# Rotary step of a second attention: the half exchange moved into the product, one addition for two, and new scheduling orders

## Chip, cores and metric

The kernel runs on one core of one Trainium2 chip. The metric is the device time of one execution in microseconds (us), the median of three runs. The profile is one further execution taken by the hardware profiler.

## What is computed

The reference handles 16 sequences of 256 tokens and 256 channels, all in float32. It adds four blocks to the input `x` in turn:

```
x = x + attention0(cross_attention(x, fside))         # 16 heads of 16, rotary, causal
x = x + feed_forward0(selected_linear(x))             # FP4-like quantisation by blocks of 16
x = x + attention1(diffusion(x))                      # 16 heads of 64, rotary, segments of 128
x = x + mixture_of_experts(conditioned(x))            # 8 experts, top 2, and a shared one
```

The change concerns the rotary step of `attention1`:

```
q = q * cos + rotate_half(q) * sin      # rotate_half: (t0, t1) -> (-t1, t0), pair by pair
k = k * cos + rotate_half(k) * sin
```

The weights are laid out so that the first elements of all pairs stand in one half (`r = 0`) and the second elements in the other (`r = 1`). With the halves a and b the result is `a*cos - b*sin` and `b*cos + a*sin`.

## The kernel before

The first three blocks are written as generators, one for each stage and engine-independent: `stage_h`, `stage_i` (cross attention), `stage_a`, `stage_m`, `stage_x`, `stage_e` (first attention), `stage_y`, `stage_f` (feed forward; `stage_gate`, `stage_up`, `stage_down` quantise its weights at the start), `stage_d` (diffusion), `stage_p`, `stage_k`, `stage_u` (queries, keys, values of the second attention), `stage_s`, `stage_g`, `stage_v` (its scores, exponentials and values). Each stage loops over the 16 sequences, and the second attention over four groups of four heads within each. The fourth block (`mixture`) is ordinary code that follows.

A planner, `weave`, interleaves the stages while the program is built. It keeps a modelled clock for each engine, asks every stage for its next operation, and issues the one that can start first. Between operations that can start equally early on the same engine, the table `ORDER` decides: it ranks the stages for each engine (PE, DVE, ACT, POOL, and SP, which issues the DMAs). So a changed cost or rank moves instructions on every engine, while their number and sizes stay the same, with two exceptions. An operation that may run on ACT or DVE (`copy_`) can change its engine. And where the modelled PE would stand idle by more than `GAP`, and a multiplication of the identity by itself into a free PSUM bank fits ahead of the next real one with a `MARGIN` of 0.2 us, the planner puts that in (`kept_warm`); its result is not used. In this text these are the fillers; in the profile they are `single<-ident` with no second operand, two matrix instructions each.

The second product and the two additions stand in `turned4`, which `stage_p` and `stage_k` call 64 times each. PE writes both halves of a projection into one bank `pq`, DVE makes `t1 = pq * cos` and `t2 = pq * sin`, both 128x512, POOL combines them in two instructions of 128x256, and SP issues four DMAs of 64 KB which bring the halves into the interleaved places of `f_q` or `keys`. `stage_s` then multiplies `f_q` and `keys` on PE. All of the woven operations carry the line L186 in the profile, that of the helper that records them; in it `single` and `pair` are PSUM tiles, `f_t1q`, `f_t2q`, `f_t1k` and `f_t2k` the products, `b_e` and `f_prob` the probabilities of the two attentions, `c_y` and `d_h` the rows that are quantised in the feed forward.

Of the kernel before, what the change touches and what calls it, by code (L numbers as in the profile page):

```python
# [13 lines left out]
F32 = mybir.dt.float32  # L14
# [3 lines left out]
ALU = mybir.AluOpType  # L18
AX = mybir.AxisListType

P = 128
S = 256
# [89 lines left out]
class Op:  # L112
# [14 lines left out]
SIDE = {32: 0.125, 64: 0.2}  # L127
TURN = 0.01
XBUFS = 7
GAP = 0.6  # L130
MARGIN = 0.2
SLACK = {"PE": 0.0, "DVE": 0.05, "ACT": 0.1, "POOL": 0.02, "SP": 0.0}
EARLY = 200.0, 0.2
EASE = 1.5
ORDER = {
    "PE": "h y down a i m f s e g v d p gate c k x u up",
    "DVE": "d v f c h i x e a g k up gate p down u s m y",
    "ACT": "f p up h i k y gate m e a v d u g x c s down",
    "POOL": "m f h i e a y v down x g s d u up gate k p c",
    "SP": "v x a h i f p g s m d gate y u up k e c down",  # L140
}
BANK_LATER = {"PE": None, "DVE": True, "ACT": True, "POOL": None, "SP": None}

# [71 lines left out]
def weave(streams, spare):  # L215
# [64 lines left out]
    while waiting:  # L280
# [36 lines left out]
        waiting = [w for w in waiting if w[0] is not None]  # L317
        if best is not None and best[2][0] == "PE" and best[2][2] and best[3] > free.get("PE", 0.0) + GAP:
            op = spare()
# [29 lines left out]
def mm_(g, out, pairs, start=True, stop=True):  # L349

    last = len(pairs) - 1
    for i, (lhsT, rhs) in enumerate(pairs):
        yield g.pe.matmul(out, lhsT, rhs, start=start and i == 0, stop=stop and i == last)


def copy_(g, dst, src):

    a, v = g.act.copy(dst, src), g.dve.tensor_copy(dst, src)
    return Op(a.choices + v.choices, a.outs, a.ins)
# [42 lines left out]
def load(g, pool, name, shape, src):  # L402

    t = pool.tile(shape, F32, name=name)
    return t, g.sp.dma_start(out=t, in_=src)
# [12 lines left out]
def single(g, *ins):  # L418

    return (yield Want(g.singles, ins))  # L420
# [269 lines left out]
def row32(j, n):  # L690
    return slice(32 * j, 32 * j + n)
# [328 lines left out]
def tile_l(g, shape, name, bufs=1, tag=None):  # L1020
    return g.l_.tile(shape, F32, name=name, tag=tag or name, bufs=bufs)


def stage_p(g):
    k, a = g.k, g.a
    yield lambda: g.done["A"] > 0 and g.done["W"] == 3 and g.done["T"] > 2 * max(OTHER) + 1


    g.z = []
    for n in ("condB_zX", "condB_zY", "condB_zR"):  # L1030
        t, op = load(g, g.w, n, [P, g.B], a[n].unsqueeze(0).to_broadcast([P, g.B]))
        g.z.append(t)
        yield op

    g.iota, op = load(g, g.w, "iota", [16, 1], a["iota"][0:16])
    yield op
    idxf = g.w.tile([16, g.B], F32, name="idxf")
    yield g.dve.tensor_copy(idxf, k.idx[0:16, 2, :])
    yield g.dve.tensor_scalar(k.onehot, idxf, g.iota, None, ALU.is_equal)

    zc = g.w.tile([P, g.B], F32, name="zc")
    yield g.dve.tensor_tensor(zc, g.z[0], g.z[1], ALU.add)
    yield g.dve.scalar_tensor_tensor(zc, zc, -2.0, g.z[2], ALU.mult, ALU.add)
    yield g.dve.tensor_scalar(g.z[2], g.z[2], -1.0, None, ALU.mult)
    g.z.append(zc)
    g.gn, op = load(g, g.w, "g", [P, 2], a["g"])
    yield op
    g.cos1, op = load(g, g.w, "cos1", [P, S], a["cos1"])
    yield op
    g.sin1, op = load(g, g.w, "sin1", [P, S], a["sin1"])  # L1050
    yield op

    g.pmo = g.w.tile([P, 2, D], F32, name="pmo")
    pmv = tile_l(g, [P, 2, 2, 2 * P], "wq", 2)
    yield g.sp.dma_start(out=pmv, in_=a["pmv"].rearrange("p c (r w) -> p c r w", r=2))
    for c in range(2):
        wo = tile_l(g, [P, 4, D], "wq", 2)
        yield g.sp.dma_start(out=wo, in_=a["w_out1"][:, 4 * c : 4 * c + 4, :])
        pmvT = tile_l(g, [P, 4, P], "f_pT", 3)
        one = yield from single(g, pmv)  # L1060
        pt = one.rearrange("p (i t) -> p i t", i=4)
        for i in range(4):
            yield g.pe.transpose(pt[:, i, :], pmv[:, c, i // 2, (i % 2) * P : (i % 2 + 1) * P], g.ident)
        yield copy_(g, pmvT, pt)
        g.singles.append(one)
        one = yield from single(g, pmvT, wo)
        pm = one[:, :D]
        yield from mm_(g, pm, [(pmvT[:, i, :], wo[:, i, :]) for i in range(4)])
        yield copy_(g, g.pmo[:, c, :], pm)
        g.singles.append(one)  # L1070

    g.keys = [g.w.tile([P, 2, 2, PM + P], F32, name=f"keys{n}") for n in range(4)]
    part = tile_l(g, [P, 2, S], "f_t1q").rearrange("p r s -> p (r s)")[:, : 8 * PM]
    part = part.rearrange("p (n a m) -> p n a m", n=4, a=2)
    for h in range(4):
        for r in range(2):
            src = a["pmk"][row32(h, 32), :, r, h * PM : (h + 1) * PM]
            dst = part[64 * (h % 2) + r : 64 * (h % 2) + 64 : 2, :, h // 2, :]
            yield g.sp.dma_start(out=dst, in_=src)
    for n in range(4):  # L1080
        yield g.pool.tensor_copy(g.keys[n][:, :, :, 0:PM], part[:, n].unsqueeze(2).to_broadcast([P, 2, 2, PM]))
    g.mhalf = g.w.tile([P, 2], F32, name="mhalf")
    yield g.pool.memset(g.mhalf, -0.5)
    g.done["Z"] = 1
    g.wq, g.queries = {0: (yield from fetch_p(g, 0))}, {}
    for i in range(4 * g.B):
        yield lambda: g.done["D"] > i // 4 and i < g.done["S"] + 2 and g.done["K"] >= i
        if i + 1 < 4 * g.B:
            g.wq[i + 1] = yield from fetch_p(g, (i + 1) % 4)
        q = g.queries[i] = tile_l(g, [P, 2, S], "f_q", 2)  # L1090
        move = lambda half, a, src: g.sp.dma_start(out=q[half, a, :], in_=src)
        yield from turned4(g, g.zT[i // 4], g.wq[i][:, 0], "q", DH1**-0.5, move)
        g.done["P"] = i + 1


def stage_k(g):

    yield lambda: g.done["Z"]
    by_seg = lambda t: t.rearrange("p (s t) -> p s t", s=2)
    for i in range(4 * g.B):  # L1100
        yield lambda: g.done["D"] > i // 4 and i < g.done["S"] + 4 and i in g.wq
        keys = g.keys[i % 4]
        move = lambda half, a, src: g.sp.dma_start(out=keys[half, a, :, PM:], in_=by_seg(src))
        yield from turned4(g, g.zT[i // 4], g.wq[i][:, 1], "k", None, move)
        g.done["K"] = i + 1
# [49 lines left out]
def fetch_p(g, n):  # L1155

    wq = tile_l(g, [P, 2, 2, 2 * P], "wq", 2)
    for which in range(2):
        cols = slice((8 * which + 2 * n) * P, (8 * which + 2 * n + 2) * P)
        yield g.sp.dma_start(out=wq[:, which], in_=g.a["w_qk1"][:, :, cols])  # L1160
    return wq
# [31 lines left out]
def turned4(g, zT, w, name, scale, move):  # L1193

    one = yield from single(g, w, zT)
    pq = one.rearrange("p (r t) -> p r t", r=2)
    for r in range(2):
        yield from mm_(g, pq[:, r, :], [(w[:, c, r * P : (r + 1) * P], zT[:, c, :]) for c in range(2)])
    t1, t2 = tile_l(g, [P, 2, S], f"f_t1{name}"), tile_l(g, [P, 2, S], f"f_t2{name}")
    for t, by in ((t1, g.cos1), (t2, g.sin1)):  # L1200
        table = by.unsqueeze(1).to_broadcast([P, 2, S])
        if scale is None:
            yield g.dve.tensor_tensor(t, pq, table, ALU.mult)
        else:
            yield g.dve.scalar_tensor_tensor(t, pq, scale, table, ALU.mult, ALU.mult)
    g.singles.append(one)
    yield g.pool.tensor_tensor(t1[:, 0, :], t1[:, 0, :], t2[:, 1, :], ALU.subtract)
    yield g.pool.tensor_tensor(t1[:, 1, :], t1[:, 1, :], t2[:, 0, :], ALU.add)
    for a in range(2):
        for r in range(2):  # L1210
            yield move(slice(r, P, 2), a, t1[64 * a : 64 * a + 64, r, :])
# [632 lines left out]
```

## Time and profile before

| | us |
|---|---|
| median of three runs (2489.93 to 2493.80) | 2491.32 |
| the profiled execution | 2491.22 |
| its span, from first to last instruction | 2489.5 |
| PE busy, share of the span | 2447.2, 98% |
| DVE, ACT, POOL busy | 1345.4, 1205.1, 1061.1 |
| end of the woven part, by its last PE instruction | 1523.6 |

The page gives busy time by engine and in 40 slices of the span. Matrix instructions overlap, and their ends are modelled; where the space from one start to the next matters, it is taken from the trace's starts. A group's line gives out<-in, shapes, count, the busy time of the group, the mean ns of one, and then the idle time of the engine ahead of them with what ended most of it.

### The profile page before, as it was taken

What the parts mean: (1) busy time and instruction counts of PE and PEld (TensorE: products, weight loads), DVE (VectorE), ACT (ScalarE), POOL (GpSimd) and SP (SyncE); (2) the same over time, 40 slices, a digit from 0 to 9 for tenths busy, and PEclk for the clock granted to TensorE, in tenths of its full rate; (3) what the DMA queues carried; (4) which work ended last, traced back from release to release, by engine and by line L of the source; (5) the groups of instructions that cost most, each with busy time, mean ns of one, the idle gap of its engine ahead of it and who ended that gap; (6) DMA issues with size and microseconds to landing.
All of it is one profiled execution on the core that took longest, in us unless ns stands there. A gap on an engine that the chain in (4) does not pass through costs nothing. (4 is left out here: it accounts for less than half of the span.)

```text
span 2489.5 us, 39426 instructions
## 1 busy us (share of the span) xinstructions
PE 2447.2 (98%) x13339; PEld 1859.7 (75%) x13339; DVE 1345.4 (54%) x2640; ACT 1205.1 (48%) x3567; POOL 1061.1 (43%) x1212
## 2 busy tenths in 40 slices
PE   8999999999999999999999999999999999999999
PEld 7776777777777777777778885555668888888866
DVE  6777877978888877888876652333300000000023
ACT  3765666666676666666664554223212322322311
POOL 6555666666666656675665442333200000000044
PEclk9999999999999999999999999999999999999999
DMA  5432332322233232222233544111224556555433
GB/s 163 145 128 80 96 103 68 100 92 73 87 93 99 73 96 83 79 88 88 83 100 118 174 136 141 51 51 51 79 81 153 198 181 201 199 185 198 155 101 108
DMA packets 229725, 285.00 MB, mean 114 GB/s; under 512 B 45233, under 2 KB 192657, under 8 KB 220177
## 3 DMA queue, kind: packets, MB, share of 16 engines
q1 hardware_dynamic: 223376, 265.66, 33.7%
q0 software_dynamic: 6144, 16.79, 2.1%
q8 instruction: 108, 1.77, 0.3%
q14 instruction: 97, 0.79, 0.1%
HBM read 210.78 MB, written 33.82 MB: 98 GB/s over the span
## 5 line engine op out<-in xcount | busy, mean ns | idle before, releaser
L1472 POOL DMA_INDIRECT got<-osort,pos_o x64 | 62.0, 968 | 628.5 <-ACT hT L1405 585.6
L1454 ACT ACTIVATE ehT<-bank,own_b 128x256 f32<-128x256 f32 x280 | 132.5, 473 | 349.1 <-PE bank L53 349.1
L53 PE MATMUL bank<-ysT,w 128*128 128x256 f32 x1120 | 247.5, 379 | 0.2 <-ACT ysT L108 0.2
L53 PE MATMUL bank<-w,ehT 128*128 128x256 f32 x1120 | 247.5, 379 | 0.0
L186 PE MATMUL single<-e_zT,wq 128*128 128x256 f32 x1024 | 243.6, 381 | 1.8 <-DMA wq<-in_w_qk 1.0
L53 PEld LDWEIGHTS bank<-ysT,w 128*128 128x128 f32 x1120 | 212.7, 190 | 29.4 <-ACT ysT L108 0.5
L53 PEld LDWEIGHTS bank<-w,ehT 128*128 128x128 f32 x1120 | 210.2, 190 | 27.2
L186 POOL TENSOR_TENSOR b_e<-b_e,b_stat 128x1024 f32<-128x1024 f32 x124 | 186.1, 1502 | 104.2 <-DVE b_stat L186 87.4
L186 ACT ACTIVATE b_e<-b_e,b_stat 128x256 f32<-128x256 f32 x496 | 220.4, 448 | 12.8 <-DVE b_stat L186 12.7
L186 ACT ACTIVATE f_prob<-f_prob,f_stat 128x144 f32<-128x144 f32 x512 | 207.6, 409 | 24.7 <-DVE f_stat L186 24.5
L186 PEld LDWEIGHTS single<-e_zT,wq 128*128 128x128 f32 x1024 | 185.7, 190 | 26.4 <-issue 2.0
L186 POOL TENSOR_TENSOR f_prob<-f_prob,f_stat 128x512 f32<-128x512 f32 x128 | 136.1, 1063 | 110.6 <-DVE f_stat L186 98.3
L1462 DVE TENSOR_TENSOR eo<-bank,eb 128x512 f32<-128x512 f32 x35 | 24.2, 692 | 234.4 <-PE bank L53 234.4
L186 ACT COPY b_pT<-single 128x512 f32<-128x512 f32 x186 | 108.2, 586 | 68.2 <-PE single L186 67.6
L1569 POOL DMA_INDIRECT ysort<-r_y,r_posi x64 | 62.4, 976 | 162.9 <-DMA ysort<-r_y,r_posi 101.7
L186 PE MATMUL single<-wo,f_oT 128*128 128x256 f32 x512 | 128.2, 383 | 0.5 <-ACT f_oT L186 0.4
L1421 DVE COPY own_b<-b1t 128x8 f32<-128x8 f32 x35 | 5.9, 174 | 222.3 <-ACT ehT L1454 222.3
L186 PE MATMUL single<-wv,e_zT 128*128 128x256 f32 x512 | 121.9, 381 | 0.0
L1405 ACT ACTIVATE hT<-bank,b 128x512 f32<-128x512 f32 x64 | 43.9, 687 | 157.4 <-PE bank L53 151.2
L186 POOL TENSOR_TENSOR f_t1q<-f_t1q,f_t2q 128x256 f32<-128x256 f32 x128 | 99.3, 791 | 41.6 <-DVE f_t2q L186 20.4
L186 PE MATMUL single<-ident,b_e 128*128 128x128 f32 x744 | 113.0, 277 | 3.4 <-POOL b_e L186 1.2
L186 DVE TENSOR_REDUCE b_stat<-b_e 128x4 f32<-128x1024 f32 (+1 forms) x124 | 114.5, 941 | 1.4 <-ACT b_e L186 0.8
(329 smaller groups left out, 5406.4 us busy)
## 6 DMA issues: line engine op xcount, KB each, us to landing
w<-in_w SPq DMA_DIRECT2D x70, 1024.0 KB
wq<-in_w_qk SPq DMA_DIRECT2D x128, 256.0 KB
wv<-in_w_v SPq DMA_DIRECT2D x64, 256.0 KB
keys<-f_t1k SPq DMA_DIRECT2D x256, 64.0 KB
f_q<-f_t1q SPq DMA_DIRECT2D x256, 64.0 KB
wo<-in_w_out SPq DMA_DIRECT2D x64, 256.0 KB
ys<-ysort SPq DMA_DIRECT2D x35, 256.0 KB
osort<-eo SPq DMA_DIRECT2D x35, 256.0 KB
```

What stands on the lines that cost most here:

```text
L53: nc.tensor.matmul(out, lhsT, rhs, start=start and i == 0, stop=stop and i == last)
L186: return Op([(self.name, self.cost(fn, outs, aps), lambda: call(*args, **kw))], outs, aps)
L1405: nc.scalar.activation(hT[:, f, :], ph, AF.Gelu_apprx_tanh, bias=k.b1[:, NE, f : f + 1])
L1421: nc.vector.tensor_copy(b1, r.b1t[:, t, :])
L1454: nc.scalar.activation(hT[:, f, :], ph, AF.Gelu_apprx_tanh, bias=b1[:, f : f + 1])
L1462: nc.vector.tensor_tensor(o, po, b2.unsqueeze(1).to_broadcast([P, 2, D]), ALU.add)
L1472: nc.gpsimd.indirect_dma_start(out=g, out_offset=None, in_=k.osort[:, :], in_offset=bass.IndirectOffsetOnAxis(ap=r.pos_o[:, i, t : t + 1], ...
L1569: nc.gpsimd.indirect_dma_start(out=k.ysort[:, :], out_offset=bass.IndirectOffsetOnAxis(ap=posi[:, i, t : t + 1], axis=0), in_=ys[t], in_of ...
```

## The change

The table of sines gets a second half of the opposite sign, made once on POOL. The second product reads the two halves of `pq` in exchanged order and multiplies by that table, so that one addition over both halves is left. `GAP` and four of the five rows of `ORDER` are new.

```
-GAP = 0.6
+GAP = 0.3
 ORDER = {
-    "PE": "h y down a i m f s e g v d p gate c k x u up",
+    "PE": "h down a i m f x s g y c e gate v d p k u up",
     "DVE": "d v f c h i x e a g k up gate p down u s m y",
-    "ACT": "f p up h i k y gate m e a v d u g x c s down",
-    "POOL": "m f h i e a y v down x g s d u up gate k p c",
-    "SP": "v x a h i f p g s m d gate y u up k e c down",
+    "ACT": "p f up k h i y gate a m e u v d g x c s down",
+    "POOL": "f m h i e a y down x g v s d u up k p gate c",
+    "SP": "v x a h i f p g gate m d s u y up e c k down",
 }
...
-    g.sin1, op = load(g, g.w, "sin1", [P, S], a["sin1"])
-    yield op
+    g.sin2 = g.w.tile([P, 2, S], F32, name="sin2")
+    yield g.sp.dma_start(out=g.sin2[:, 1, :], in_=a["sin1"])
+    yield g.pool.tensor_scalar(g.sin2[:, 0, :], g.sin2[:, 1, :], -1.0, None, ALU.mult)
...
-    for t, by in ((t1, g.cos1), (t2, g.sin1)):
-        table = by.unsqueeze(1).to_broadcast([P, 2, S])
+    for t, by, src in ((t1, g.cos1.unsqueeze(1).to_broadcast([P, 2, S]), pq), (t2, g.sin2, pq[:, ::-1, :])):
         if scale is None:
-            yield g.dve.tensor_tensor(t, pq, table, ALU.mult)
+            yield g.dve.tensor_tensor(t, src, by, ALU.mult)
         else:
-            yield g.dve.scalar_tensor_tensor(t, pq, scale, table, ALU.mult, ALU.mult)
+            yield g.dve.scalar_tensor_tensor(t, src, scale, by, ALU.mult, ALU.mult)
     g.singles.append(one)
-    yield g.pool.tensor_tensor(t1[:, 0, :], t1[:, 0, :], t2[:, 1, :], ALU.subtract)
-    yield g.pool.tensor_tensor(t1[:, 1, :], t1[:, 1, :], t2[:, 0, :], ALU.add)
+    yield g.pool.tensor_tensor(t1, t1, t2, ALU.add)
```

## Prediction

> **What bounds the kernel now.** I read the page first, then a table of stretches, then PE's waits, then the groups that the change touches, and last the starts of the matrix instructions one by one.
>
> ```profile
> span 2489.5 us, 39426 instructions
> PE 2447.2 (98%) x13339; PEld 1859.7 (75%) x13339; DVE 1345.4 (54%) x2640; ACT 1205.1 (48%) x3567; POOL 1061.1 (43%) x1212
> PEclk9999999999999999999999999999999999999999
> ```
>
> PE is busy all through at full clock; no other engine is near. The table of stretches (PE, PEld, DVE, ACT, POOL busy) shows where PE is not:
>
> ```profile
> 0.00:78.00 78.00, 68.23 (x453) 58.73 (x453) 54.99 (x100) 34.48 (x98) 47.58 (x59) 1.00 0.49 160
> 78.00:160.00 82.00, 79.52 (x463) 59.59 (x464) 60.65 (x113) 57.32 (x185) 42.23 (x41) 1.00 0.44 143
> 160.00:300.00 140.00, 134.34 (x807) 99.64 (x806) 107.10 (x193) 83.22 (x266) 79.24 (x86) 1.00 0.30 91
> 300.00:1400.00 1100.00, 1088.13 (x6830) 821.99 (x6829) 874.77 (x1525) 706.77 (x2333) 695.50 (x796) 1.00 0.31 93
> 1400.00:1524.00 124.00, 122.14 (x785) 95.22 (x784) 60.01 (x110) 66.25 (x222) 53.26 (x93) 1.00 0.39 116
> ```
>
> The woven part ends at 1524 us; the mixture behind it (965 us) is not changed. In the woven part PE is idle for 1524 - 1492.4 = 31.6 us, a third of it before 78 us. DVE is busy 76% of it and POOL 60%. So time is lost or won here only through PE: its real work, which the change leaves as it is, the fillers, and the waits. What PE waits for (total us, times, longest):
>
> ```profile
> PE single L186 <- POOL d_h L186: 3.3, 6, 0.9
> PE single L186 <- POOL c_y L186: 2.3, 3, 1.1
> PE pair L186 <- POOL f_v L186: 2.2, 1, 2.2
> PE pair L186 <- POOL b_diag L186: 1.3, 4, 0.4
> PE single L186 <- POOL b_e L186: 1.2, 3, 0.7
> PE single L186 <- DVE f_t2k L186: 0.5, 2, 0.3
> ```
>
> Many causes, none large. After 160 us they sum to 18.7 us, of which 9.6 us in 21 waits name POOL as the one that came last. No wait names the DMAs that carry the turned queries or keys to their tiles; the rotary step runs far enough ahead.
>
> **The rotary edit.**
>
> ```profile
> L186 POOL TENSOR_TENSOR f_t1q<-f_t1q,f_t2q 128x256 f32<-128x256 f32 x128 | 99.3, 791 | 41.6 <-DVE f_t2q L186 20.4 <-DVE f_stat L186 12.1 <-issue 7.3
> L186 POOL TENSOR_TENSOR b_qk<-b_t,b_t 128x512 f32<-128x512 f32 x32 | 41.0, 1283 | 37.9 <-DVE b_t L186 26.4 <-DVE f_stat L186 9.3 <-DVE b_stat L186 1.5
> L186 DVE SCALAR_TENSOR_TENSOR f_t2q<-single,sin 128x512 f32<-128x512 f32 x64 | 43.4, 677 | 0.0
> L186 PE MATMUL single<-ident 128*128 128x128 f32 x400 | 55.8, 285 | 1.7 <-POOL ident masks.py:199 1.6 <-DVE f_t2k L186 0.2
> ```
>
> POOL: 256 additions of 0.79 us (99.3 + 98.7 = 198.0 us) become 128 of 128x512. The same operation at that shape is the `b_qk` row, 1.283 us, so 164.2 us: POOL is relieved of 33.8 us, 0.26 us in each step. What is this worth? Each of PE's 21 waits on POOL after 160 us can shrink by at most 0.26, together 5.5 us, and by nothing if no rotary addition stood ahead in POOL's queue. Rotary additions are 198 of POOL's 918 us, 22%, so I take 0.22 x 5.5 = 1.2 us.
>
> On the other side stands the queue that issues the four DMAs. By the starts in the trace, the first DMA of a query goes out 0.03 us after the first addition, the second 0.03 after the second, the third and fourth 0.57 and 1.22 after it. From the start of the additions (two of 0.73 with 0.04 saved in the overlap: 1.42) the last goes out at 1.42 + 1.22 = 2.64 us. With one addition the first cannot go before 1.28, and then four follow at 0.6 to 0.64 each: the last at 1.28 + 0.03 + 1.87 = 3.18. The step gets 0.54 us longer to the scores, though POOL works less. SP's later issues stand behind it, by the same amount. The cover is the PE work between a step's projection and its scores: by the listing of instruction order, priced with the trace, at least 5.7 us, median 16.7, in the changed program; two of 64 places have under 8, about what products, additions and DMAs take. Two times 0.54 = 1.1 us, at most 64 times 0.54 if all cover were gone, which no wait of before suggests. The two effects cancel: -0.1.
>
> DVE: the second product keeps its count and size. What it reads in exchanged halves no row shows; the nearest are the products of the first attention that read the other element of each pair (724 and 558 ns against 677). That bounds it to between -119 and +47 ns, times 128 between -15 and +6 us of DVE time, off PE's path. I take 0, as each half is still read as one unbroken run of 256.
>
> The new table costs POOL one instruction, between 0.37 (128x44) and 0.79 us. In the listing it stands ahead of the first `c_xT`. Behind it wait `c_xT` and with it the first gate products. In the trace POOL sits idle there:
>
> ```profile
> 120.00 1.27 POOL L186 TENSOR_TENSOR f_q<-wo,f_pm 128x512 f32<-128x512 f32 x1
> 124.69 1.06 POOL L186 TENSOR_TENSOR c_xT<-c_y,q_inv_y 128x512 f32<-128x512 f32 x1 [3.42 <-DVE b_stat L186]
> ```
>
> The load of the table is issued at 118.06, and 3.42 us are free: 0. Were the cover gone it would cost its own 0.8 us, once.
>
> **The fillers.** The listing of both programs gives the same PE operations but for fillers: 200 before, 259 after. Starts within a run of fillers lie 112 ns apart, so one filler (two instructions) takes 0.224 us: +59 are 13.2 us of PE, if nothing else moves. They split in two. A listing with `GAP` alone lowered has 245, the other operations in the same order. So I can look up each of the 45 places in the trace of before: how much later than one interval did the next real instruction start? Full 0.224 us free at 23 places, part at 9, nothing at 13. Before 78 us: 20 fillers, 4.5 us, 2.7 of them into idle time; the other 1.8 lie ahead of the 2.2 us wait for `f_v`, whose chain starts at loads, and vanish there (if that cover goes, +1.8). After: 25 fillers, 5.6 us, 3.6 into idle time, **2.0 us left**. The new orders add the other 14, from the third sequence on, in the start and in the last 200 us. Whether such a gap is real or not, PE spends the time: 14 x 0.224 = **3.1 us**, unless waits go elsewhere.
>
> Do they? I compared in the listings, for sixteen kinds of chain, the PE work between producer and consumer with what the chain between takes by the rows. Shortfalls: 50 places, 29.5 us before; 49 places, 26.6 us after. No sign of a better or worse order beyond 2.9 us, and I take 0.
>
> Do fillers buy clock? In the trace, fillers start 213 ns apart until 5.1 us and 112 ns afterwards; after the longest later wait (2.24 us, at 78 us) the starts keep their usual 216 ns. So no gap that a new filler closes (0.4 to 0.6 us) costs clock now, and I take no gain. [...] Were each of the 45 gaps to cost clock instead, the fillers would win time; no row shows it.
>
> Sum: -0.1 + 0 + 2.0 + 3.1 = +5.0 us. The profiled execution took 2491.22 (span and 1.7 around it), 0.1 from the median: **2496.2 us**. A measurement tells about 0.2% (5 us) from no change, and this lies on that bound.
>
> **Rivals.**
> *The new orders close waits (faster).* Everything after 160 us that PE waits for is 18.7 us. If two thirds go, 12.5, the sum is 5.0 - 12.5 = -7.5: 2484. For it: on PE, y and e stand behind s and g now, the shortfall is 2.9 us smaller, POOL is freer. Against: 14 more fillers mean that the planner itself sees no fewer gaps. It decides from 10 us of waits removed.
> *The quantised rows come late (slower).* The waits for `d_h` and `c_y` are the largest. From gate to down the chain crosses DVE, POOL, ACT, DVE, POOL in 8.7 us of durations, and the listing leaves as little as 7.5 and 8.5 us of PE work over it where before left 9.1. With half a microsecond lost at each of the 32 quantisations of `d_h` it is +16; 6 of the 13 us of fillers would then stand in real waits, so 5 + 16 - 6 = +15: 2506. It decides once the waits for `d_h` and `c_y` pass 10 us.
> *Nothing moves.* All fillers fall into idle time: 2491.
>
> **Numbers.** Forecast 0.45, own range 2492 to 2501; faster rival 0.28, 2480 to 2486; slower rival 0.25, 2501 to 2514; nothing moves 0.02. The range 2481 to 2510 leaves some of both ends out. The forecast halves at 2496.3, so slower is 0.23 + 0.25 = 0.48, same 0.22 + 0.02 + 0.01 = 0.25, faster 0.27.
>
> **What would show it.** `f_t1q` with 64 additions near 1.28 us; `f_t2q` near 677 ns; the last query DMA about 1.9 us after its addition; `single<-ident` x518; the woven part ending near 1529 us; the mixture's 965 us unchanged; PE's waits after 160 us near 19 us. The prediction is wrong if these waits differ from it by more than 8 us either way, if the second product takes over 800 ns, or if a wait names the DMAs into `f_q` or `keys`.

## The result and the profile after

| | before | after |
|---|---|---|
| median, us | 2492.56 (2489.93 to 2495.80) | 2510.77 (2508.06 to 2512.65) |
| the profiled execution, us | 2491.22 | 2512.65 |
| its span | 2489.5 | 2510.9 |
| end of the woven part, by the start of its last PE instruction | 1523.6 | 1545.5 |
| from there to the last PE instruction | 961.4 | 960.9 |

The ratio is 1.0072 [1.0054, 1.0089]: slower, 18 us where 5 were forecast, and just outside the range of 2481 to 2510. All of it lies in the woven part. The page of after begins:

```profile
span 2510.9 us, 39376 instructions
PE 2464.0 (98%) x13457; PEld 1877.4 (75%) x13457; DVE 1351.1 (54%) x2645; ACT 1199.4 (48%) x3562; POOL 1036.0 (41%) x1085
PEclk9999999999999999999999999999999999999999
```

PE is the bound as before: 118 more matrix instructions, the 59 fillers, and 16.8 us more busy time. POOL has 25.1 us less to do, and the kernel is slower all the same. The table of stretches for after (length, then PE, PEld, DVE, ACT, POOL busy, then the granted clock, DMA share and GB/s) shows in which part the time goes:

```profile
0.00:78.00 78.00, 72.49 (x492) 63.15 (x492) 53.57 (x97) 33.87 (x96) 46.96 (x58) 1.00 0.47 157
78.00:160.00 82.00, 80.10 (x470) 61.54 (x471) 60.44 (x114) 53.48 (x169) 39.92 (x40) 0.98 0.45 143
160.00:300.00 140.00, 137.39 (x851) 103.40 (x850) 109.64 (x193) 82.97 (x273) 79.08 (x79) 1.00 0.29 88
300.00:1400.00 1100.00, 1076.99 (x6720) 810.82 (x6717) 873.85 (x1518) 698.33 (x2317) 671.17 (x689) 1.00 0.30 89
1400.00:1546.00 146.00, 142.74 (x926) 114.04 (x924) 66.36 (x123) 73.69 (x245) 55.57 (x83) 1.00 0.44 130
```

In the first 300 us PE is idle less than before. The loss is in the long even stretch from 300 to 1400 us: 23.0 us idle where before had 11.9, with 110 fewer matrix instructions done in the same 1100 us. The clock of 0.98 in the second row is told of below. PE's waits of after, from 160 us to the end of the woven part (total us, times, longest):

```profile
PE single L186 <- POOL d_h L186: 5.0, 5, 1.4
PE single L186 <- DVE x L186: 3.2, 4, 1.4
PE single L186 <- POOL b_e L186: 2.5, 3, 1.3
PE pair L186 <- POOL b_diag L186: 2.4, 5, 1.3
PE single L186 <- DVE d_th L186: 2.4, 2, 1.9
PE single L186 <- DVE f_t2k L186: 1.9, 3, 0.9
PE pair L186 <- DVE f_prob L186: 1.8, 1, 1.8
```

Before, in the same part, the largest wait of each of the two engines POOL and DVE was:

```profile
PE single L186 <- POOL d_h L186: 2.4, 5, 0.7
PE single L186 <- DVE x L186: 1.2, 1, 1.2
```

There are fewer waits, but longer ones. They sum to 28.2 us over seventeen causes, 18.7 before. Those that name POOL went from 9.6 us to 10.6, those that name DVE from 3.8 to 10.6. No stage stands out, and no wait names the DMAs into `f_q` or `keys`. The groups of the edit:

```profile
L186 POOL TENSOR_TENSOR f_t1q<-f_t1q,f_t2q 128x512 f32<-128x512 f32 x64 | 84.8, 1325 | 46.3 <-DVE f_t2q L186 18.6 <-DVE f_stat L186 16.2 <-issue 6.9
L186 DVE SCALAR_TENSOR_TENSOR f_t2q<-single,sin 128x512 f32<-128x512 f32 x64 | 43.3, 676 | 0.0
L186 PE MATMUL single<-ident 128*128 128x128 f32 x518 | 69.5, 284 | 1.6 <-POOL ident masks.py:199 1.6
```

The starts of PE's woven instructions, one after the other, give an account of the 21.9 us by which the woven part grew. Each space from one start to the next is put down to the instruction that began it. Fillers hold 72.3 us instead of 64.3 (+8.0), waits behind them included. The real instructions, as many in both, hold 1471.6 us instead of 1457.7 (+13.9). Up to 5.1 us of this execution's growth is lost to a lower clock, of which more below.

### The profile page after: what moved, and what is told of

Read it like the earlier page. It is cut to its first block, busy times and chain, and to the rows that moved or that the text cites. A ratio compares the mean times of both kernels' runs of the same rounds, so it can differ in the third digit from the quotient of the medians.

```text
span 2510.9 us, 39376 instructions
## 1 busy us (share of the span) xinstructions
PE 2464.0 (98%) x13457; PEld 1877.4 (75%) x13457; DVE 1351.1 (54%) x2645; ACT 1199.4 (48%) x3562; POOL 1036.0 (41%) x1085
## 3 DMA queue, kind: packets, MB, share of 16 engines
q8 instruction: 109, 1.79, 0.3%
## 5 line engine op out<-in xcount | busy, mean ns | idle before, releaser
L186 ACT ACTIVATE b_e<-b_e,b_stat 128x256 f32<-128x256 f32 x496 | 219.8, 448 | 14.3 <-DVE b_stat L186 11.9
L53 PE MATMUL bank<-yT,w1s 128*128 128x512 f32 x256 | 113.3, 600 | 2.0 <-DVEq L1377 2.0
```

The costliest lines, as they stand in the source:

```text
L53: nc.tensor.matmul(out, lhsT, rhs, start=start and i == 0, stop=stop and i == last)
L186: return Op([(self.name, self.cost(fn, outs, aps), lambda: call(*args, **kw))], outs, aps)
```

## The experiments

All fifteen kernels compute the whole reference. The expectations name their theories by letters. F: the fillers of the lower `GAP` take PE's time. R: the rotary step with one addition brings its four DMAs later to the scores. P: the new plan moves work on all engines, and other waits arise; O is P narrowed to the new ranks in `ORDER`. L, formed after the second set: any new plan loses against the old one, whatever caused it to be made, since the old plan is one that happens to suit the chip. Kernels that begin with a are made from after, with b from before.

**One part at a time.** Every set was run in rounds together with before, and the ratios are to before's runs of the same set. Five rounds, before at 2492.35.

`b_gap3` is before with the lower threshold alone; its other instructions keep before's order, and 45 fillers are added.

```
-GAP = 0.6
+GAP = 0.3
```

> The kernel before with GAP alone at 0.3: its orders, 45 fillers more. P and R: +2 to +4 us, 2494 to 2497, by the idle time found at the 45 places. F: +8 us or more, over 2500.

Measured: 2493.34, 1.0007 [0.9998, 1.0015], +1.7 us. The interval, from -0.5 to +3.7 us, holds the 2.0 of the place-by-place count, and also nothing at all. F, with 8 us or more, falls for this plan.

`a_gap6` is after with `GAP = 0.6`; the other instructions keep after's order, 44 fillers go.

> The changed kernel with the threshold back at 0.6: every engine's order as in the changed kernel, 44 fillers fewer. Theory P (the new plan makes new waits; the fillers cost what the prediction said): 3 to 5 us faster than the changed kernel, about 2506. Theory F (the fillers themselves hold the matrix work up): most of the 18 us come back, 2495 to 2500. Theory R (the one addition, with its later DMAs, holds buffers and queues): like P, 2506.

Measured: 2503.40, 1.0057 [1.0043, 1.0071]. So the threshold gives back 0.15 of the 0.72%, and the intervals overlap. The time lies between the 2506 of P and R and the 2500 of F. Most of the loss is there with before's own threshold; F alone can't be the cause. The stretch of its profile from 300 to 1400 us has PE idle for 22.9 us, as after:

```profile
300.00:1400.00 1100.00, 1077.07 (x6727) 812.01 (x6726) 876.69 (x1514) 699.79 (x2324) 672.88 (x690) 1.00 0.31 90
```

`b_merged` is the other half of the question: the changed arithmetic in before's plan. The planner is given the old two additions at their old prices; the first issues nothing, the second issues the merged one. (The half table is made beside a later POOL instruction in the same way; that part of the edit isn't shown.) In the traces PE, DVE and ACT run the same instructions in the same order as in before.

```
-    yield g.pool.tensor_tensor(t1[:, 0, :], t1[:, 0, :], t2[:, 1, :], ALU.subtract)
-    yield g.pool.tensor_tensor(t1[:, 1, :], t1[:, 1, :], t2[:, 0, :], ALU.add)
+    first = g.pool.tensor_tensor(t1[:, 0, :], t1[:, 0, :], t2[:, 1, :], ALU.subtract)
+    first.choices = [(*first.choices[0][:2], lambda: None)]
+    yield first
+    op = g.pool.tensor_tensor(t1[:, 1, :], t1[:, 1, :], t2[:, 0, :], ALU.add)
+    op.choices = [(*op.choices[0][:2], lambda: g.k.nc.gpsimd.tensor_tensor(t1, t1, t2, ALU.add))]
+    yield op
```

> The kernel before with the changed rotary arithmetic (exchanged halves, table of both signs, one addition at the place of the second), all orders as before: the rotary edit alone, with no new plan. R: slower by 8 us or more, over 2500. P and F: within 3 us of 2492, as the prediction's -0.1 for the rotary edit says.

Measured: 2494.17, 1.0012 [1.0003, 1.0022], +3.0 us for the rotary edit in the old plan. Its stretch from 300 to 1400 us, and its additions, which carry a line of their own, as the helper doesn't issue them:

```profile
300.00:1400.00 1100.00, 1086.84 (x6818) 820.73 (x6810) 880.38 (x1527) 708.34 (x2340) 675.31 (x695) 1.00 0.31 92
L1218 POOL TENSOR_TENSOR f_t1q<-f_t1q,f_t2q 128x512 f32<-128x512 f32 x64 | 85.1, 1330 | 24.0 <-DVE f_t2q L186 21.2 <-issue 1.1 <-POOL f_pm L186 1.0
```

The addition takes 1330 ns here and 1325 in after, but PE is idle for 13.2 us here and for 23.0 there. The instruction is the same, the place it stands in differs.

`a_split` is after with the merged addition issued as two of 128x256 in the same place, so that the first two DMAs can leave after the first.

```
-    yield g.pool.tensor_tensor(t1, t1, t2, ALU.add)
+    op = g.pool.tensor_tensor(t1, t1, t2, ALU.add)
+
+    def halves():
+        for r in range(2):
+            g.k.nc.gpsimd.tensor_tensor(t1[:, r, :], t1[:, r, :], t2[:, r, :], ALU.add)
+
+    op.choices = [(*op.choices[0][:2], halves)]
+    yield op
```

> The changed kernel with the one addition of 128x512 issued as two of 128x256 at the same place; all orders on the other engines are the same, so the first DMA of a step may go out 0.5 us earlier and POOL works 0.2 to 0.3 us more in each step. R: faster by 8 us or more, under 2503. P and F: within 3 us of the changed kernel's 2510.8.

Measured: 2506.99, 1.0065 [1.0051, 1.0078]. In its trace the first DMA of a query leaves 0.76 us after the additions' start and the last 2.68 us, both medians; in after these are 1.31 and 3.16 us. So half a microsecond is won at the middle step, yet the time can't be told from after's. It lies 3.8 us under after's median, outside both expectations (within 3 us, or under 2503). With `b_merged` beside it, R is no more than a small part.

What is left is P: with the arithmetic of after, the old plan costs 0.12% and the new plan, at the same threshold, 0.57%.

**Which part of the planner's input.** Three rounds, before at 2491.36. The four kernels keep `GAP = 0.6`. `rot_only` has the changed rotary step with before's ranks. `ord_only` has before's rotary step with the new ranks. `pe_new` is `rot_only` with the new row for PE, `pe_old` is `a_gap6` with the old row for PE:

```
-    "PE": "h y down a i m f s e g v d p gate c k x u up",
+    "PE": "h down a i m f x s g y c e gate v d p k u up",
```

> The changed rotary step with the ORDER and GAP of before, planned anew (196 fillers). Theory O (the new ranks make the loss): 2491 to 2496, as the kernel before. Theory L (any new plan misses the tuned one by luck, whatever ranks it has): 2498 or more, or as far on the other side.

> The kernel before with the new ORDER alone, its own rotary step and GAP 0.6, planned anew (251 fillers). O: 2500 to 2510, as the changed kernel with GAP 0.6 (2503.4). L: anywhere, but not tied to the changed kernel's loss. If the ranks only harm together with the new rotary step, 2492 to 2496.

> The changed rotary step with GAP 0.6 and the ORDER of before, but for the new PE row (207 fillers). If PE's ranks are the part of O that counts (they start rows of sequence b later and move the quantised rows of the feed forward): 2500 to 2505. If it is the rows of ACT, POOL and SP: 2491 to 2496.

> The changed kernel with GAP 0.6 and the old PE row, the other new rows kept (186 fillers, the fewest of all). If PE's ranks count: 2488 to 2496. If the rows of ACT, POOL and SP count: 2500 to 2505.

| | rotary step | ranks | us | ratio |
|---|---|---|---|---|
| `rot_only` | new | old | 2505.93 | 1.0059 [1.0042, 1.0076] |
| `a_gap6` | new | new | 2503.40 | 1.0057 [1.0043, 1.0071] |
| `ord_only` | old | new | 2527.89 | 1.0138 [1.0121, 1.0155] |
| `pe_new` | new | old, PE new | 2500.84 | 1.0037 [1.0026, 1.0048] |
| `pe_old` | new | new, PE old | 2502.77 | 1.0043 [1.0026, 1.0060] |

(The second row is from the set before, beside its own runs of before.) O falls: with the new rotary step the new ranks change nothing that can be measured, 1.0059 against 1.0057. Nor do the parts add up: the new ranks alone cost 1.38%, more than all together. And by their expectations `pe_new` speaks for PE's row and `pe_old` for the others, which can't both be. What the five have in common is only that the planner made a new plan.

**A new plan for no reason.** Three rounds, before at 2490.83. If L holds, a nudge of a price that the planner uses, with no change to what is computed, to a rank or to the threshold, must cost as much. Each of three kernels raises the fixed price of one engine's instructions by under 1% (us; the second number is per element):

```
-COSTS = {"DVE": (0.15, 0.00105), "ACT": (0.16, 0.00083), "POOL": (0.30, 0.0016)}
+COSTS = {"DVE": (0.15, 0.00105), "ACT": (0.16, 0.00083), "POOL": (0.302, 0.0016)}   # b_pool302
+COSTS = {"DVE": (0.151, 0.00105), "ACT": (0.16, 0.00083), "POOL": (0.30, 0.0016)}   # b_dve151
+COSTS = {"DVE": (0.15, 0.00105), "ACT": (0.161, 0.00083), "POOL": (0.30, 0.0016)}   # b_act161
```

The rival was that the planner has a wrong price for the merged addition, 1.12 us where the median in after's trace is 1.28. `rot_cost` is `rot_only` with the measured price:

```
-    yield g.pool.tensor_tensor(t1, t1, t2, ALU.add)
+    op = g.pool.tensor_tensor(t1, t1, t2, ALU.add)
+    op.choices = [(op.choices[0][0], 1.28, op.choices[0][2])]
+    yield op
```

> The kernel before, its arithmetic, ORDER and GAP untouched; only the planner's fixed price of a POOL instruction is 0.302 us for 0.300, so that it plans anew (216 fillers). Theory L (the old plan is one that fits the chip by selection, and any other plan loses, whatever the reason for it): 2498 to 2512. Theory O/R (ranks or the rotary step make the loss): 2489 to 2496.

> The same with the fixed price of a DVE instruction at 0.151 for 0.150 us (204 fillers). L: 2498 to 2512. O/R: 2489 to 2496.

> The same with the fixed price of an ACT instruction at 0.161 for 0.160 us (226 fillers). L: 2498 to 2515. O/R: 2489 to 2496.

> The changed rotary step with the ORDER and GAP of before, the one addition planned at 1.28 us, as the trace has it, in place of the planner's 1.12 (203 fillers). If the loss of the new plan comes from that wrong price: 2490 to 2498. L: like the same kernel planned with 1.12 (2505.9), 2498 to 2512.

Measured: `b_pool302` 2501.91, 1.0041 [1.0027, 1.0055]; `b_dve151` 2503.45, 1.0043 [1.0029, 1.0057]; `b_act161` 2502.51, 1.0042 [1.0027, 1.0056]; `rot_cost` 2497.02, 1.0022 [1.0012, 1.0032]. The three nudged kernels have before's arithmetic, ranks and threshold, and each loses 0.4%. `rot_cost` came out in the range of the wrong price, under that of L. The stretch of `b_dve151` from 160 to 1400 us, and under it the largest of PE's waits there and up to the end of its woven part:

```profile
160.00:1400.00 1240.00, 1215.98 (x7559) 916.81 (x7558) 973.11 (x1701) 788.73 (x2603) 764.80 (x877) 1.00 0.30 90
```

```profile
PE single L186 <- POOL d_h L186: 5.3, 5, 2.3
PE single L186 <- DVE x L186: 2.9, 4, 0.9
PE single L186 <- DVE f_t2q L186: 2.4, 3, 1.7
PE single L186 <- POOL b_e L186: 2.2, 3, 1.2
```

PE is idle for 24.0 us in this stretch; in before the rows of 160 to 300 and of 300 to 1400 us give 17.5. The list looks like after's, `d_h`, `x` and `b_e` among the first, in a program whose rotary step is before's. The three differ in their waits after 160 us: `b_pool302` puts 14.3 us on POOL and 4.6 on DVE, `b_dve151` 12.0 and 7.8, `b_act161` 5.9 and 9.0. In `b_act161` two waits of 2.6 us together name the DMAs into `keys`, with before's rotary step.

**Is the price the cure?** `rot_cost` lost least, so the wrong price could still be a cause beside L. Three rounds, before at 2489.47: `rot_cost_d` and `rot_cost_p` are `rot_cost` with one of the nudges each (DVE 0.151, POOL 0.302), `a_cost6` is `a_gap6` with the measured price.

> The changed rotary step, ORDER and GAP of before, addition planned at 1.28 us, and DVE's fixed price nudged from 0.150 to 0.151 (234 fillers). If the true price is what helped: 2493 to 2500. If 2497 was one draw of a spread: as likely over 2500, 2500 to 2512.

> The same with POOL's fixed price nudged from 0.300 to 0.302 instead (207 fillers; the addition stays at 1.28). True price: 2493 to 2500. Spread: 2500 to 2512 as likely as not.

> The changed kernel with GAP 0.6 and the addition planned at 1.28 us, under the new ORDER (247 fillers; with 1.12 it had 215 and took 2503.4). True price: 2494 to 2500. Spread: 2500 to 2520; with 32 fillers more rather on the upper side.

Measured: `rot_cost_d` 2527.25, 1.0153 [1.0130, 1.0176]; `rot_cost_p` 2509.95, 1.0079 [1.0062, 1.0096]; `a_cost6` 2516.11, 1.0102 [1.0085, 1.0119]. With the right price four plans lie between 2497 and 2527, as wide as all plans without it (2501 to 2528): the price is no cure, and `rot_cost` was a good draw. `rot_cost_d` even lies beyond the spread that was expected. Two stretches of `rot_cost_d`, the second just past the end of its woven part at 1561 us, and then its largest waits of PE after 160 us:

```profile
300.00:1400.00 1100.00, 1073.52 (x6721) 806.79 (x6722) 880.32 (x1507) 697.03 (x2307) 661.83 (x684) 1.00 0.29 87
1400.00:1564.00 164.00, 155.92 (x979) 122.50 (x978) 77.04 (x136) 76.46 (x254) 66.11 (x91) 0.99 0.44 131
```

```profile
PE single L186 <- POOL d_h L186: 5.5, 5, 1.8
PE single L186 <- POOL c_y L186: 4.8, 6, 1.1
PE single L186 <- DVE x L186: 4.6, 6, 1.1
```

The long stretch loses 26.5 us, more than after's, and from 1400 us to the end of the woven part it needs 161 us, where before needs 124. Again the loss is spread over many waits.

**What the plans have in common.** Twelve different new plans were run at the threshold of 0.6, and all twelve lose against before's, by 0.22 to 1.53%. The count of fillers, that is of gaps that the planner itself sees, tells only the worst: the three plans with 234 to 251 took 2516 to 2528, the nine with 186 to 226 took 2497 to 2510 in no order (196 gave 2506, 203 gave 2497). By the same account of PE's starts, the real instructions hold between 4.6 us (`rot_cost`) and 25.7 us (`rot_cost_d`) more than in before. So before's plan is better than all twelve draws in something that the planner's model doesn't show it. That this plan was once picked for its time on the chip would explain this, but is only argued.

What the planner's model misses wasn't isolated. One wait of `a_gap6` shows a candidate. Its timeline (start, duration, engine, instruction; in brackets what ended the engine's idle time):

```profile
978.10 3.42 DVE L186 SCALAR_TENSOR_TENSOR q_xn<-q_big,q_xn 128x704 f32<-128x704 f32 x2
979.08 1.69 POOL L186 TENSOR_TENSOR b_e<-b_e,b_stat 128x512 f32<-128x512 f32 x1
981.66 1.39 POOL L186 TENSOR_TENSOR d_h<-q_xn,q_scl 128x704 f32<-128x704 f32 x1 [0.89 <-DVE q_xn L186]
983.10 0.66 PE L186 MATMUL single<-ident,d_h 128*128 128x128 f32 x4 [1.45 <-POOL d_h L186]
```

Two DVE instructions of 128x704, 0.89 us each at the median in before and after, take 3.42 us together here while POOL works on `b_e`; `d_h` comes that much later, and PE waits 1.45 us. In the traces of before and after every one over 894 ns ran beside a POOL instruction: the 30 of 64 in after with none beside them take 877 to 893 ns, the 34 beside one from 884 up to 1845, and 18 of those over 1200; in before it is 27 with 879 to 894 ns and 37 with 879 up to 2394, 19 of them over 1200. The planner's price depends on the instruction alone, and not on what POOL does meanwhile. But the 64 take nearly as long together in before as in after (69.1 and 71.3 us). So it is where the long ones fall, not how many there are, that could differ, and no run varied that alone. Whether this makes the loss stays open.

No version faster than before was found; the best with the changed step is `b_merged`, in the old plan, at 1.0012.

## Why the prediction was wrong

**What bounds it: right.** PE, 98% busy, and the mixture behind the woven part unchanged (961.4 and 960.9 us).

**POOL's relief: half wrong.** The median merged addition takes 1276 ns, as the row of `b_qk` promised. The mean is 1325 (1354 for the keys), since some take up to 2012, so POOL saves 26.5 us and not 33.8. No gain on PE is seen: the waits that name POOL are 10.6 us where 9.6 were, and 8.4 were expected.

**The DMAs: right for after, wrong for before, the sum too low.** First and last DMA of a query leave 1.31 and 3.16 us after the addition's start (predicted 1.31 and 3.18). But the 2.64 us that the prediction worked out for the last one before holds only for the quickest quarter of the steps. The median there is 3.16 too, and the mean falls from 3.78 to 3.50 us. So the first DMA leaves 0.55 us later, and the last, at the middle step, no later: the term of 0.54 us for each step isn't there in this form. The net of -0.1 us for the rotary edit measured +3.0 [+0.7, +5.5] in `b_merged`. Executions with a mean granted clock of 0.999 differ by less, 2493.5 (6 of `b_merged`) against 2492.0 (28 of before). No wait names these DMAs in after, and one of 0.3 us in `b_merged`; in `rot_only` five do, 2.0 us together. What made up the 3 us wasn't taken apart further.

**The second product and the table: right.** 676 ns against 677 with the halves in exchanged order; no wait names the table.

**The threshold: near in the old plan, in part by luck.** +1.7 us measured for 2.0, in an interval that holds 0. Executions of `b_gap3` with a mean clock of 0.999 and 1.000 took 2.3 and 3.8 us more than before's with the same; the medians are closer because fewer of its executions had a low clock, a difference that may be chance. In the new plan it is 0.15%, some 4 us, with overlapping intervals. The 59 extra fillers hold 8.0 us more of PE's start-to-start time; the sum had 5.1.

**The plan: the step that failed.** "Do they?" compared, for sixteen kinds of chain, the work on PE between producer and consumer with the durations of the chain, found 49 places with 26.6 us instead of 50 with 29.5, and said "No sign of a better or worse order beyond 2.9 us, and I take 0". The runs put 0.45% there, about 11 us: from `b_merged` (1.0012) to `a_gap6` (1.0057), with the same work and threshold. At a mean clock of 0.999 they took 2493.5 (6 executions) and 2503.1 (3), so the clock doesn't explain it. PE's idle time after 160 us rose by 9.5 us (19.4 to 28.9 by the records of PE alone) from before to after, while the shortfall fell. The comparison took every chain as if its engines were free for it, and each instruction at its mean. It couldn't see an instruction that waits in DVE's or POOL's queue behind other stages, nor one that takes twice its median. The waits that name DVE, 3.8 us before and 10.6 after, may be of that sort; no run separates the two, and which chains the comparison had wrong stays open. A second plan of known time would have put it to the test beforehand, and there was none.

**The clock: wrong in its reason, small in its size.** The prediction read from the 2.24 us wait at 78 us that gaps of this length cost no clock. The profile of after has two records of half clock in the woven part, of 3.4 and 6.8 us, and before's has none there. If PE was busy all through them, 5.1 us are lost, an estimate; that counts in the account above. But this differs from one execution to the next, in before too: over its 58 executions beside these kernels, the 18 with a mean granted clock of 1.000 took 2489.3 us on average, the 6 with 0.997 took 2496.1. At an equal mean clock of 0.999, before took 2492.0 (28 executions) and after 2509.9 (3), so the clock doesn't explain the 18 us. The profiled execution, with 0.997, is the longest of after's four.

**The rivals.** The slower one gave 2506, the nearest number, and its range of 2501 to 2514 holds the measured time, but by luck: it decides once the waits for `d_h` and `c_y` pass 10 us, and after 160 us they went from 4.7 to 5.0. The faster one needed 10 us of waits less; there are 9.5 more. The bound that the prediction set for itself, waits off by over 8 us, is passed.

## What to carry to other kernels

When a planner builds the order, an edit is two changes: the work, and the new plan. Measure the edit in the frozen old plan, and measure the new plan by itself with a control that nudges a price and computes the same; here the control cost 0.4%, over three times the edit's 0.12%. Where one plan has beaten every draw, a static look at chains doesn't tell what leaving it costs; put the spread of nudged plans into the forecast, or keep the plan.

## What was not expected of the hardware

In the woven part of after the clock fell to half twice: for 3.4 us at 80.40 us, 1.05 us behind the end of a wait of 2.02 us, and for 6.8 us at 548.03 us, within a wait of 1.79 us. The two places in the stretches of after, each with the 3.4 us ahead of the half-clock stretch (columns as above; the clock is the third number from the right, 1.00 or 0.50), and from the timeline the wait that ended at the second:

```profile
77.00:80.40 3.40, 1.38 (x8) 1.11 (x8) 3.37 (x6) 1.17 (x2) 1.92 (x4) 1.00 0.35 113
80.40:83.80 3.40, 3.40 (x14) 2.94 (x13) 2.62 (x4) 1.49 (x6) 2.13 (x4) 0.50 0.00 0
544.60:548.00 3.40, 1.45 (x4) 0.68 (x4) 3.40 (x7) 2.43 (x12) 3.29 (x3) 1.00 0.13 34
548.00:551.40 3.40, 3.12 (x20) 2.52 (x22) 3.40 (x8) 0.58 (x1) 2.39 (x3) 0.50 0.25 63
```

```profile
548.28 1.33 PE L186 MATMUL pair<-keys,f_q 64*128 64x144 f32 x8 [1.79 <-DVE f_prob L186]
```

PE was busy for 1.38 and 1.45 of the 3.4 us ahead, 41 and 43%, with no single wait over 2.02 us. In the profile of before the wait at 78 us is longer, 2.24 us, and it lies across these two stretches, with PE busy for 2.23 and 2.33 us of 3.40:

```profile
73.50:76.90 3.40, 2.23 (x22) 2.04 (x18) 3.26 (x4) 0.86 (x5) 2.53 (x3) 1.00 0.71 213
76.90:80.30 3.40, 2.33 (x13) 2.11 (x14) 3.40 (x6) 2.26 (x6) 2.63 (x5) 1.00 0.21 67
```

The clock stayed full. So in these two profiles the length of the longest wait alone doesn't tell where the clock fell; what does wasn't settled. The 3.4 us at half clock cost up to half their length, 1.7 us, an estimate that takes PE as busy all through them. Four such losses would make the 6.8 us between before's executions with mean clocks of 1.000 and 0.997; the change cost 18.
